# Projection bias as a plain load added by VectorE, last two norms' sums by accumulating operations with squares on ScalarE

## The chip, the cores and the metric

The kernel runs on one core of one Trainium2 chip. The metric is device time in microseconds (us), each version beside the kernel before on the same chip. TensorE is called PE in profiles, PEld is its weight load, VectorE is DVE, ScalarE is ACT, GpSimd is POOL, SyncE is SP.

## The reference, cut to what matters

128 samples of 128 rows by 512 columns go through a max over a small graph product and a norm, then through attention with 8 heads, a projection with bias, a norm, a residual, and a last norm:

```python
x = _layernorm(x + relu_max(adj, x, b))            # layer 0: "first norm"
qkv = x @ w_qkv                                    # 12 "products" per group of 4 samples
o = softmax(mask(q k^T * scale)) v @ w_proj + b_proj
ln = (o - mu) * rsqrt(var + eps) * ln_gamma + ln_beta
x = _layernorm(x + o + ln)                         # needs the sums of o, then of x + o + ln
```

In these inputs `b_proj` and `ln_beta` are zero and `ln_gamma` is one, but a general kernel must apply them.

## The kernel before

A group is four samples; there are 32. TensorE does a **dense stretch** (products 4 to 11, which give q and k, and one projection), then an **attention stretch** (scores, transposes, attend, projections, and the v products). Every operation has a place in a plan, in us. TensorE and ScalarE run in exactly the plan's order; the order on VectorE, GpSimd and SyncE is left to the scheduler. To **evacuate** a product is to read it out of the buffer that TensorE wrote it to (a PSUM buffer), so that the next product can use it: ScalarE reads the main part, then VectorE adds the rest. A wait in an engine's queue holds up what stands behind it: in group 13 below ScalarE is idle for 2.49 us while a finished product stands behind the operation that waits.

```python
def projected_main(b):                       # ScalarE evacuates the main part
    os[b] = work.tile([P, D], FP, tag="o", bufs=4, ...)
    nc.scalar.activation(os[b], pps["o", b][0], AF.Copy, scale=1.0 + 1.0 / HALF)   # last group: VectorE
def projected_rest(b):
    nc.vector.tensor_tensor(os[b], os[b], pps.pop(("o", b))[1], op=ALU.add)
def bias(b):                                 # GpSimd: accumulating DMA
    nc.gpsimd.dma_start(os[b], row(b_proj), accum_op=ALU.add)
def residual_beta(b):                        # xb: 3 buffers, loaded with x by SyncE before
    nc.gpsimd.dma_start(xbs[b], row(ln_beta), accum_op=ALU.add)
def residual_o(b):
    nc.gpsimd.dma_start(xbs[b], os[b], accum_op=ALU.add)
def stats(mv, src, name):                    # VectorE
    nc.vector.bn_stats(st, src)
    nc.vector.bn_aggr(mv, st)
# then GpSimd: add eps, power -0.5; VectorE: norm_1; stats again; ScalarE: norm_2; store
def dense_main(g, j):                        # evacuation of product j: ScalarE, then VectorE
    nc.scalar.activation(dense_to(g, j), pps[g, j][0], AF.Copy, scale=1.0 + 1.0 / HALF)
def dense_rest(g, j):
    nc.vector.tensor_tensor(dst, dst, pps.pop((g, j))[1], op=ALU.add)
# [cut: loads, splits into high and low parts, softmax, plan]
```

## Time and profile before

| | before |
|---|---|
| median, fastest to slowest of 3 | 2183.7 us, 2180.96 to 2185.78 |
| TensorE busy | 2073.4 us, 95% |
| group 2's start, 28 groups from there, the rest | 146.6, 1867.2, 177.3 us |
| mean group | 66.69 us |

All but the first row are of the profiled execution, which took 2192.8 us, 0.4% above the median.

The busy shares make TensorE the bound. What is left to win without taking matmuls away lies in its idle gaps and in matmuls that run slowly after a gap. The prediction shows the lines and reads them.

### The profile page before, as it was taken

The numbers are of one execution on the slowest core, as the hardware profiler recorded it, in microseconds if no ns is written. First come the engines' busy times: TensorE is split into PE (matmuls) and PEld (weight loads), VectorE is DVE, ScalarE is ACT, GpSimd is POOL, SyncE is SP. The second block draws the span as 40 slices with busy tenths as digits, with TensorE's granted clock in tenths as the row PEclk, the third lists the DMA queues.
The fourth block names the chain that finished last, engine by engine and source line by source line (L and its number), as shares of the span: only waits on it lengthen the run. The fifth ranks groups of instructions, "written<-read, shape, count | busy, mean of one in ns | idle before, by whom it ended". The sixth has DMA issues, their size and how long they took to land.

```text
span 2191.1 us, 34777 instructions
## 1 busy us (share of the span) xinstructions
PE 2073.4 (95%) x12033; PEld 1612.2 (74%) x12033; DVE 1726.7 (79%) x2747; ACT 1334.3 (61%) x3742; POOL 719.0 (33%) x1325
## 2 busy tenths in 40 slices
PE   7899999999999999999999999999999999999986
PEld 5677777777777777777777777777777777777764
DVE  7688777887778887778877788877788877788876
ACT  5756565665656666666656566666566666566652
POOL 2122334323343233343223332333332233332334
PEclk8999999999999999999999999999999999999998
DMA  5135455344554454554444544544544454544443
GB/s 179 58 71 118 110 121 121 82 107 111 120 117 90 114 119 111 121 121 86 113 111 116 124 87 111 119 114 116 127 90 107 119 113 120 129 90 102 104 99 90
DMA packets 134000, 239.85 MB, mean 109 GB/s; under 512 B 14656, under 2 KB 18880, under 8 KB 133824
## 3 DMA queue, kind: packets, MB, share of 16 engines
q0 software_dynamic: 54144, 98.59, 27.5%
q1 hardware_dynamic: 79392, 138.97, 19.6%
q8 instruction: 95, 1.56, 0.3%
q14 instruction: 81, 0.66, 0.1%
q10 hardware_dynamic: 288, 0.07, 0.0%
HBM read 137.95 MB, written 67.11 MB: 94 GB/s over the span
## 4 chain that ended last, share of the span: by engine, by line
PE 47%; DMA 18%; POOL 13%; DVE 10%; ACT 7%; issue 5%; POOLq 0%; SPq 0%; DVEq 0%; ACTq 0%
DMA o<-in_L_gnn_b_proj_dram 14%; PE psc L324 5%; ACT e L346 4%; PE ppt L361 4%; DMA xb<-x 3%; POOL rstd L168 3%; PE pav L374 3%; PE pa L189 2%; PE ptx L245 2%; POOL xb L418 2%; POOL ve L166 2%; DVE o L432 2%; POOL ssq L227 1%; DVE st L179 1%; POOL sum L213 1%
## 5 line engine op out<-in xcount | busy, mean ns | idle before, releaser
L346 ACT ACTIVATE e<-e,nmax 128x128 f32<-128x128 f32 x1024 | 395.6, 390 | 1.6 <-DVE nmax L339 1.5
L410 POOL DMA_DIRECT2D o<-in_L_gnn_b_proj_dram x124 | 114.4, 923 | 633.7 <-DVE o L405 609.2
L418 POOL DMA_DIRECT2D xb<-o x124 | 110.2, 889 | 428.1 <-DMA o<-in_L_gnn_b_proj_dram 428.1
L432 DVE SCALAR_TENSOR_TENSOR o<-o,rstd,xb 128x512 f32<-128x512 f32 x128 | 96.0, 750 | 175.7 <-POOL rstd L168 175.5
L365 ACT COPY eT<-ppt 128x1024 f32<-128x1024 f32 x128 | 128.9, 1007 | 127.8 <-PE ppt L361 127.8
L265 ACT CAST x_h<-xh 128x512 fp32r<-128x512 f32 x128 | 79.4, 621 | 188.9 <-DVE xh L253 188.3
L346 ACT ACTIVATION_READ_ACCUMULATOR e<-e,nmax 128x1 f32 x1024 | 193.9, 189 | 0.0
L389 POOL DMA_DIRECT2D xb<-in_L_gnn_ln_beta_dram x128 | 119.2, 931 | 224.4 <-DMA xb<-x 111.0
L331 DVE SCALAR_TENSOR_TENSOR e<-psc,mask 128x1024 f32<-128x1024 f32 x128 | 156.0, 1219 | 43.9 <-PE psc L324 43.9
L234 ACT ACTIVATE xt<-xt,sum,ssq 128x512 f32<-128x512 f32 x128 | 97.1, 805 | 139.1 <-POOL sum L228 139.1
L179 DVE BATCH_NORM_STATS2 st<-o 128x6 f32<-128x512 f32 x256 | 173.3, 678 | 9.5 <-DMA o<-in_L_gnn_b_proj_dram 6.2
L218 ACT ACTIVATE square<-xt,sum 128x512 bf16<-128x512 f32 x128 | 92.1, 719 | 115.4 <-POOL sum L213 113.4
L361 PEld LDWEIGHTS ppt<-ident,e 128*128 128x128 f32 x1024 | 119.8, 141 | 52.4 <-issue 46.5
L355 DVE TENSOR_TENSOR e<-e,sums 128x1024 f32<-128x1024 f32 x128 | 155.4, 1214 | 0.1
L339 DVE TENSOR_REDUCE nmax<-e 128x8 f32<-128x1024 f32 x128 | 154.8, 1209 | 0.0
L168 POOL TENSOR_TENSOR rstd<-ve,mhalf 128x1 f32<-128x1 f32 x256 | 150.4, 589 | 10.5
L324 PE MATMUL psc<-qkT 64*128 64x128 f32 x2048 | 149.1, 285 | 2.7 <-DVE qkT L313 2.7
L324 PEld LDWEIGHTS psc<-qkT 64*128 64x128 f32 x2048 | 124.4, 188 | 25.9 <-issue 15.6
L374 PE MATMUL pav<-eT,v 128*64 128x128 f32 x2048 | 140.1, 279 | 1.2 <-ACT eT L365 1.2
L374 PEld LDWEIGHTS pav<-eT,v 128*64 128x64 f32 x2048 | 109.2, 136 | 41.9 <-issue 29.0
L189 PE MATMUL pa<-xt,adjT 128*128 128x512 f32 x256 | 135.6, 616 | 0.4 <-DVE adjT L99 0.4
L361 PE MATMUL ppt<-ident,e 128*128 128x128 f32 x1024 | 132.9, 273 | 0.5 <-DVE qkT L313 0.5
(4652 smaller groups left out, 5681.8 us busy)
## 6 DMA issues: line engine op xcount, KB each, us to landing
xt<-in_x_dram SPq DMA_DIRECT2D x128, 256.0 KB, 2.9
x<-xt SPq DMA_DIRECT2D x128, 256.0 KB, 2.6
xb<-x SPq DMA_DIRECT2D x128, 256.0 KB, 3.5
xb<-in_L_gnn_ln_beta_dram POOLq DMA_DIRECT2D x128, 256.0 KB, 5.5
out_dram<-o SPq DMA_DIRECT2D x128, 256.0 KB, 3.8
o<-in_L_gnn_b_proj_dram POOLq DMA_DIRECT2D x124, 256.0 KB, 4.2
xb<-o POOLq DMA_DIRECT2D x124, 256.0 KB, 3.3
wraw<-in_L_gnn_w_qkv_dram SPq DMA_DIRECT2D x12, 256.0 KB, 3.7
```

Source lines behind the costliest of these rows:

```text
L168: nc.gpsimd.tensor_tensor(r, ve, mhalf[:, :n], op=ALU.pow)
L179: nc.vector.bn_stats(st, src)
L189: nc.tensor.matmul(pa[b], adjT, xs[b], start=True, stop=True)
L324: nc.tensor.matmul(psc[:, s, hp, :], qkT[hs, hp, i, :], qkT[hs, KC + hp, i, :], start=True, stop=True,)
L331: nc.vector.scalar_tensor_tensor(e, pscs.pop(b).rearrange("p s a m -> p (s a) m"), scale, mask_b, op0=ALU.mult, op1=ALU.add,)
L339: nc.vector.tensor_reduce(nmax, es[b], AX.X, ALU.max, negate=True)
L346: nc.scalar.activation(e[:, j, :], e[:, j, :], AF.Exp, bias=nmax[:, j : j + 1], accum_out=sums[:, j : j + 1],)
L355: nc.vector.tensor_tensor(e, e, sums[:, :, None].to_broadcast([P, H, P]), op=ALU.mult)
L361: nc.tensor.transpose(ppts[b][:, j, :], e[:, j, :], ident)
L374: nc.tensor.matmul(pavs[b][s * HD : (s + 1) * HD, hp, :], v[:, h * HD : (h + 1) * HD], eT[:, s * HP + hp, :], start=True, stop=True,)
L418: nc.gpsimd.dma_start(xbs[b], os[b], accum_op=ALU.add)
L432: nc.vector.scalar_tensor_tensor(o, o, norms.pop((b, 1)), xbs.pop(b), op0=ALU.mult, op1=ALU.add,)
```

## The change

Intent: take the bias off GpSimd's queue, which stands still until each accumulating load has landed, and take the statistics off VectorE. The sum comes with an operation that runs anyway, and the sum of squares is made by ScalarE as (sum - 512 x)^2, so no mean is needed first. The norms get new places.

```diff
-    def projected_main(b):   # ScalarE copy, bias later by GpSimd
+    def bias(b):
+        os[b] = work.tile([P, D], FP, tag="o", bufs=4, name=f"o_{b}")
+        nc.sync.dma_start(os[b], row(b_proj))
+    def projected_main(b):
+        nc.vector.scalar_tensor_tensor(
+            os[b], pps["o", b][0], 1.0 + 1.0 / HALF, os[b], op0=ALU.mult, op1=ALU.add)
     def projected_rest(b):
-        nc.vector.tensor_tensor(os[b], os[b], pps.pop(("o", b))[1], op=ALU.add)
+        add_sum(b, 1, pps.pop(("o", b))[1], 1.0, os[b])      # same, with accum_out
+    def squares(x, s):
+        nc.scalar.activation(square, x, AF.Square, bias=s[:, 0:1], scale=-float(D), accum_out=s[:, 1:2])
+    def deviation(s, n):                                     # GpSimd
+        nc.gpsimd.tensor_scalar(s, s, float(D) ** -3, EPS, op0=ALU.mult, op1=ALU.add)
+        nc.gpsimd.tensor_tensor(s, s, mhalf[:, :n], op=ALU.pow)
-    stats_1, stats_2 by bn_stats and bn_aggr                 # [cut]
+    stats(b, 1), stats(b, 2) by squares and deviation        # [cut]; the first norm's too
-        at(u + 3.0, bias, b)
+        at(u - 5.0, bias, b)
 # [cut: keep_0, mean_0, rstd_0, load_bias]
-                at(u + 9.0 + 1.0 * i, norm_0, b + i)
+                at(u + 14.0 + 1.5 * i, norm_0, b + i)
-                u = t + (10.0 + 5.0 * i if g < NG - 1 else (4.0, 9.0, 14.0, 27.6)[i])
-                normed((g - 2) * G + i, u, u + 2.0, u + 3.5, u + 6.0)
+                u = t + 1.0 + 4.5 * i
+                normed((g - 2) * G + i, u, u + 3.0, u + 6.0, u + 9.0)
```

The four arguments of `normed` after the sample are the places of the first statistics, norm_1, the second statistics and norm_2. For the fourth sample of a group (i = 3), norm_2 now stands at t + 23.5.

More of the change, by code (lines that the diff above doesn't have):

```diff
@@ L81, in tile_adj_resnorm_d2 @@
     pps, qkTs, vs, pscs, es, ppts, eTs = {}, {}, {}, {}, {}, {}, {}
-    pavs, oTs, xbs, os, mv1s, norms = {}, {}, {}, {}, {}, {}
+    pavs, oTs, xbs, os, sums_of, norms = {}, {}, {}, {}, {}, {}
     def load_x(b):
@@ L161, in load_gamma @@
         nc.sync.dma_start(gamma_sb, row(ln_gamma))
-    def norm_of(mv, n, name):
-        ve = small.tile([P, n], FP, tag=f"ve{n}", name=f"ve_{name}")
-        nc.gpsimd.tensor_scalar(ve, mv[:, :, 1], EPS, None, op0=ALU.add)
-        r = small.tile([P, n], FP, tag=f"rstd{n}", name=f"rstd_{name}")
-        nc.gpsimd.tensor_tensor(r, ve, mhalf[:, :n], op=ALU.pow)
-        return r
-    def shift_of(mv, r, n, name):
-        nm = small.tile([P, n], FP, tag=f"nm{n}", name=f"nm_{name}")
-        nc.gpsimd.tensor_scalar(nm, mv[:, :, 0], -1.0, None, op0=ALU.mult)
-        nc.gpsimd.tensor_tensor(nm, nm, r, op=ALU.mult)
-        return nm
-    def stats(mv, src, name):
-        st = small.tile([P, 6], FP, tag="bnst", name=f"st_{name}")
-        nc.vector.bn_stats(st, src)
-        nc.vector.bn_aggr(mv, st)
     def conv(b):
@@ L203, in add_0 @@
         if i == 0:
-            mv0s[g] = [small.tile([P, G], FP, tag=f"{n}0", bufs=2, name=f"{n}0_{g}") for n in ("sum", "ssq")]
+            mv0s[g] = small.tile([P, G, 3], FP, tag="sum0", bufs=2, name=f"sum0_{g}")
         nc.scalar.activation(
-            xs[b], xs[b], AF.Identity, bias=rms[g][:, i : i + 1], accum_out=mv0s[g][0][:, i : i + 1],
+            xs[b], xs[b], AF.Identity, bias=rms[g][:, i : i + 1], accum_out=mv0s[g][:, i, 0:1],
         )
-    def mean_0(b, n):
-        g, i = divmod(b, G)
-        m = mv0s[g][0][:, i : i + n]
-        nc.gpsimd.tensor_scalar(m, m, -1.0 / D, None, op0=ALU.mult)
     def stats_0(b):
         g, i = divmod(b, G)
-        nc.scalar.activation(
-            square, xs[b], AF.Square, bias=mv0s[g][0][:, i : i + 1],
-            accum_out=mv0s[g][1][:, i : i + 1],
-        )
+        squares(xs[b], mv0s[g][:, i, :])
     def rstd_0(b, n):
         g, i = divmod(b, G)
-        nmean, ssq = (m[:, i : i + n] for m in mv0s[g])
-        nc.gpsimd.tensor_scalar(ssq, ssq, 1.0 / D, EPS, op0=ALU.mult, op1=ALU.add)
-        nc.gpsimd.tensor_tensor(ssq, ssq, mhalf[:, :n], op=ALU.pow)
+        total, ssq, nmean = (mv0s[g][:, i : i + n, k] for k in range(3))
+        nc.gpsimd.tensor_scalar(nmean, total, -1.0 / D, None, op0=ALU.mult)
+        deviation(ssq, n)
         nc.gpsimd.tensor_tensor(nmean, nmean, ssq, op=ALU.mult)
@@ L393, in project @@
         product(("o", b), b % G != 0, lambda kc: [(f[:, kc, :], w[:, kc, :]) for f, w in parts])
+    def bias(b):
+        os[b] = work.tile([P, D], FP, tag="o", bufs=4, name=f"o_{b}")
+        nc.sync.dma_start(os[b], row(b_proj))
     def projected_main(b):
-        os[b] = work.tile([P, D], FP, tag="o", bufs=4, name=f"o_{b}")
-        if b < B - G:
-            nc.scalar.activation(os[b], pps["o", b][0], AF.Copy, scale=1.0 + 1.0 / HALF)
-        else:
-            nc.vector.scalar_tensor_tensor(
-                os[b], pps["o", b][0], 1.0 + 1.0 / HALF, xs["bias"], op0=ALU.mult, op1=ALU.add,
-            )
-    def projected_rest(b):
-        nc.vector.tensor_tensor(os[b], os[b], pps.pop(("o", b))[1], op=ALU.add)
-    def bias(b):
-        if b < B - G:
-            nc.gpsimd.dma_start(os[b], row(b_proj), accum_op=ALU.add)
-    def load_bias():
-        xs["bias"] = xpool.tile([P, D], FP, tag="xt", name="bias")
-        nc.sync.dma_start(xs["bias"], row(b_proj))
+        nc.vector.scalar_tensor_tensor(
+            os[b], pps["o", b][0], 1.0 + 1.0 / HALF, os[b], op0=ALU.mult, op1=ALU.add,
+        )
+    def projected_rest(b):
+        add_sum(b, 1, pps.pop(("o", b))[1], 1.0, os[b])
     def residual_o(b):
@@ L418, in residual_o, with add_sum, stats @@
             nc.gpsimd.dma_start(xbs[b], os[b], accum_op=ALU.add)
-    def stats_1(b):
-        mv1s[b] = small.tile([P, 1, 2], FP, tag="mv1", name=f"mv1_{b}")
-        stats(mv1s[b][:, 0, :], os[b], f"1_{b}")
-        norms[b, 1] = norm_of(mv1s[b], 1, f"1_{b}")
+    def add_sum(b, n, in0, scalar, in1):
+        s = sums_of[b, n] = small.tile([P, 3], FP, tag=f"sum{n}", name=f"sum{n}_{b}")
+        nc.vector.scalar_tensor_tensor(
+            os[b], in0, scalar, in1, op0=ALU.mult, op1=ALU.add, accum_out=s[:, 0:1],
+        )
+        nc.gpsimd.tensor_scalar(s[:, 2:3], s[:, 0:1], -1.0 / D, None, op0=ALU.mult)
+    def squares(x, s):
+        nc.scalar.activation(
+            square, x, AF.Square, bias=s[:, 0:1], scale=-float(D), accum_out=s[:, 1:2],
+        )
+    def deviation(s, n):
+        nc.gpsimd.tensor_scalar(s, s, float(D) ** -3, EPS, op0=ALU.mult, op1=ALU.add)
+        nc.gpsimd.tensor_tensor(s, s, mhalf[:, :n], op=ALU.pow)
+    def stats(b, n):
+        s = sums_of[b, n]
+        squares(os[b], s)
+        deviation(s[:, 1:2], 1)
+        if n == 2:
+            nc.gpsimd.tensor_tensor(s[:, 2:3], s[:, 2:3], s[:, 1:2], op=ALU.mult)
     def norm_1(b):
-        o = os[b]
+        o, s, xb = os[b], sums_of.pop((b, 1)), xbs.pop(b)
         if b >= B - G:
-            nc.vector.tensor_tensor(xbs[b], xbs[b], o, op=ALU.add)
+            nc.vector.tensor_tensor(xb, xb, o, op=ALU.add)
         nc.vector.scalar_tensor_tensor(
-            o, o, mv1s.pop(b)[:, 0, 0:1], gamma_sb, op0=ALU.subtract, op1=ALU.mult,
+            o, o, s[:, 2:3], gamma_sb, op0=ALU.add, op1=ALU.mult,
         )
-        nc.vector.scalar_tensor_tensor(
-            o, o, norms.pop((b, 1)), xbs.pop(b), op0=ALU.mult, op1=ALU.add,
-        )
-    def stats_2(b):
-        mv = small.tile([P, 1, 2], FP, tag="mv2", name=f"mv2_{b}")
-        stats(mv[:, 0, :], os[b], f"2_{b}")
-        rstd = norm_of(mv, 1, f"2_{b}")
-        norms[b, 2] = rstd, shift_of(mv, rstd, 1, f"2_{b}")
+        add_sum(b, 2, o, s[:, 1:2], xb)
     def norm_2(b):
         o = os.pop(b)
-        rstd, nm = norms.pop((b, 2))
-        nc.scalar.activation(o, o, AF.Identity, bias=nm, scale=rstd)
+        s = sums_of.pop((b, 2))
+        nc.scalar.activation(o, o, AF.Identity, bias=s[:, 2:3], scale=s[:, 1:2])
         nc.sync.dma_start(out[b], o)
@@ L463, in normed @@
         at(u - 4.0, residual_o, b)
-        at(u, stats_1, b)
+        at(u, stats, b, 1)
         at(v, norm_1, b)
-        at(w, stats_2, b)
+        at(w, stats, b, 2)
         at(z, norm_2, b)
@@ L529, in beside_dense @@
                 at(u + 5.0 + 0.9 * i, stats_0, b + i)
-            at(u + 4.5, mean_0, b, G)
-            at(u + 8.0, rstd_0, b, G)
+            at(u + 8.7, rstd_0, b, G)
             for i in range(G):
-                at(u + 9.0 + 1.0 * i, norm_0, b + i)
-                at(u + 10.0 + 1.0 * i, keep_0, b + i)
+                at(u + 14.0 + 1.5 * i, norm_0, b + i)
+                at(u + 15.0 + 1.5 * i, keep_0, b + i)
         for i in range(G):
@@ L549, in tile_adj_resnorm_d2 @@
         at(u + 2.9, add_0, b)
-        at(u + 3.3, mean_0, b, 1)
         at(u + 3.6, stats_0, b)
@@ L568, in tile_adj_resnorm_d2 @@
     at(places[3 * KC - 1], load_gamma)
-    at(PERIOD * (NG - 1), load_bias)
     t = 0.0
```

## The prediction

> **What bounds the kernel now.** I read the page's busy shares first, then who waited for whom, then one group of four samples in order of time, then a table by stage.
>
> ```profile
> PE 2073.4 (95%) x12033; PEld 1612.2 (74%) x12033; DVE 1726.7 (79%) x2747; ACT 1334.3 (61%) x3742; POOL 719.0 (33%) x1325
> ...
> POOL xb L418 <- DMA o<-in_L_gnn_b_proj_dram: 428.1, 124, 5.0
> ...
> DVE o L432 <- POOL rstd L168: 175.5, 93, 4.9
> ACT xt L234 <- POOL sum L228: 139.1, 31, 5.2
> ...
> ACT square L218 <- POOL sum L213: 113.4, 33, 4.9
> ```
>
> TensorE is busy 95% of the span, so there is little to win unless its busy time itself is inflated. The waits show a chain that starts at a transfer: GpSimd adds the projection bias with an accumulating DMA (line 410), then issues the residual DMA that reads the result (line 418), and for that it stands still until the bias has landed: 428.1 / 124 = 3.45 us each time. Everything behind it in GpSimd's queue, the small mean and rstd operations, is late; VectorE waits for rstd and ScalarE for the sums.
>
> Does it reach TensorE? Group 15 in order of time says yes:
>
> ```profile
> 1034.42 0.87 POOL L418 DMA_DIRECT2D xb<-o  x1 [4.62 <-DMA o<-in_L_gnn_b_proj_dram]
> ...
> 1037.15 0.53 POOL L168 TENSOR_TENSOR rstd<-ve,mhalf 128x1 f32<-128x1 f32 x1
> ...
> 1039.01 0.75 DVE L432 SCALAR_TENSOR_TENSOR o<-o,rstd,xb 128x512 f32<-128x512 f32 x1 [4.66 <-POOL rstd L168]
> ...
> 1040.40 0.67 DVE L313 TENSOR_TENSOR qkT<-qkT,pp_(15, 6)_10008 128x512 f32<-128x512 f32 x1
> ...
> 1041.13 0.76 PE L278 MATMUL pp_(15, 10)_10140<-x_h,w_h 128*128 128x512 f32 x1 [3.42 <-DVE qkT L313]
> 1041.69 0.63 PE L279 MATMUL pp_(15, 10)_10140<-x_l,w_l 128*128 128x512 f32 x1
> ```
>
> Read it downwards: GpSimd waits 4.62 us for the bias, so rstd comes late, so VectorE's norm waits 4.66 us, so the evacuation of product 6 is late, so product 10, which needs its PSUM buffer, keeps TensorE idle 3.42 us. Then the next matmuls follow each other at 0.43 us (1041.69 to 1042.12) where undisturbed ones take 0.233 us (1035.68 to 1035.91): the stall is paid twice.
>
> By stage, for an undisturbed attention stretch between two dense stretches:
>
> ```profile
> 952.20:979.80 27.60, 25.86 (x110) 20.39 (x109) 18.99 (x35) 17.83 (x45) 15.39 (x30) 1.00 0.55 123
> 979.80:1017.50 37.70, 37.70 (x268) 29.25 (x267) 33.93 (x51) 23.33 (x73) 6.31 (x11) 1.00 0.46 107
> 1017.50:1048.30 30.80, 27.38 (x110) 21.52 (x109) 19.34 (x35) 17.82 (x45) 16.90 (x34) 0.94 0.54 127
> ...
> 146.60:2013.80 1867.20, 1802.34 (x10531) 1405.70 (x10529) 1482.56 (x2353) 1153.00 (x3249) 625.71 (x1148) 0.99 0.49 111
> ```
>
> Columns: window, its length, then busy time of PE, PEld, DVE, ACT, POOL, the clock, DMA share, GB/s. The attention stretch is pure TensorE: 37.70 busy of 37.70. The dense stretch is not: 27.6 to 30.8 us long for at least 25.86 us of matmuls (nine products of twelve matmuls at 0.233 = 25.2, plus the 0.7 that the first one takes longer). From the first matmul of group 2's dense stretch (146.6) to group 30's (2013.8) lie 28 groups in 1867.2 us, 66.69 each; the floor is 25.86 + 37.70 = 63.56. So 28 x 3.13 = **87.5 us** are lost, of which 1867.2 - 1802.3 = 64.9 is idle TensorE and the other 22.6 us slow matmuls. Group 30 loses another 1.6. That is the whole pool from which this change can gain in the steady part: about 89 us, 4.1% of 2183.7.
>
> **What the Trainium skill says.** (1) "DMA: Bandwidth & Descriptors", section on the anatomy of one DMA from GpSimd: DMA engines do not wait on semaphores, the wait happens on the issuing sequencer before dispatch. The trace agrees: line 418's wait is GpSimd's own idle time. The same section fits about 2.0 us + bytes/436e3, 2.6 us for 256 KB; the trace's median for the bias is 4.2 us, and that decides. (2) "TensorE: Matmul & The Clock Gate", Part 1: an idle window of about 3.4 us halves the clock. The trace agrees: after 3.42 us idle the spacing nearly doubled, while after 1.74 us (group 14, product 10) it stayed at 0.23. (3) "ScalarE: Activation LUTs", rules for kernel authors: about 0.3 us per ACTIVATE plus 0.83 ns an element, 0.72 us for 512; the squares on line 218 take 0.719. (4) "VectorE: DVE Perf Modes", section on two Vector instructions with no wait between them: an operation that also writes out its accumulator is two instructions. No VectorE operation of this kernel does so; on ScalarE the read shows as 0.19 us of its own.
>
> **The change, part by part.** Consecutive records overlap, so I count by the distance between starts.
>
> *Bias.* Removed: 124 accumulating DMAs on GpSimd with 0.92 us of issue each (114 us, 3.7 per group), and with them line 418's 428 us of waiting. Added: 128 plain loads of the same 256 KB on SyncE, five places ahead of the product. A plain load from DRAM lands in 2.9 to 3.7 us in the trace, so each should be there in time, and DMA engines are at some 45% share.
>
> *Evacuation.* 124 copies leave ScalarE (0.5 us apart: 2.0 us per group) and go to VectorE as the scalar_tensor_tensor that the last group has now (line 400, 0.69 long, 0.60 apart): +2.4 us per group.
>
> *Statistics.* VectorE loses 8 bn_stats and 8 bn_aggr per group, 0.61 + 0.10 apart: -5.7 us. It gains 8 accumulator reads; I estimate 0.1 us of spacing each, as bn_aggr has: +0.8. VectorE net: 2.4 - 5.7 + 0.8 = -2.5, from 52.9 (19.0 + 33.9 above) to 50.4 us of a 63.56 us group. ScalarE gains 8 squares at 0.85 us (square and read): +6.8, less 2.0, so 41.2 to 46.0 us per group. Nearly all of the 6.8 falls in the dense stretch, where it goes from 17.8 to about 24 of 25.9 us. GpSimd's small operations stay about as many.
>
> *First norm.* The squares no longer wait for a mean from GpSimd (113 us of ScalarE waits at line 218; 4 waits of 0.34 to 0.80 at the start, which I take as 1.5 us off the start). norm_0 moves five places later, so rstd has more time before ScalarE's fixed order reaches it.
>
> None of the saved work is itself on the path, because TensorE sets the end. What counts is that GpSimd stops blocking. A product can be evacuated about 11.2 - 2.8 - 0.6 = 7.8 us late before TensorE notices (four products of PSUM buffers at 2.8 us, less its own product and evacuation), so waits of 2 or 3 us that remain cost nothing.
>
> What can remain: three xb buffers serve four samples, so the fourth's residual load, beta (5.5 us) and residual_o (3.3 us) come one after another inside the dense stretch, and GpSimd still waits there for beta to land. I estimate 0.4 us of TensorE time per group, 12 us in all. The last 115 us have 12 us of idle TensorE in waits on other engines; the bias leaves most of it, the squares add ScalarE hops to it: 0.
>
> Sum: 2183.7 - 89 + 12 - 1.5 = 2105; I say **2106 us**, 3.6% faster.
>
> **Rivals.** *ScalarE becomes the bound of the dense stretch.* For it: about 24 of 25.9 us, in a fixed order that now holds waits for VectorE and GpSimd between the evacuations of the products. Against: by my count of its order it falls some 3.5 us behind by the middle and catches up before the end, inside the 7.8 us. If it fails, each group keeps 1 to 2 us of stall: 2135 to 2160. *Another wait replaces the bias wait on GpSimd.* For it: beta is still accumulated, line 389 already waits 111 us for the residual load, and residual_o now follows beta alone. If half of the stall stays: about 2145. *VectorE in the attention stretch becomes late*, 33.9 of 37.7 busy and three more evacuations in it, or waiting for a bias that SyncE issued late. Against: the statistics of earlier samples leave that stretch, and the projection's PSUM buffer is needed again some 4 us after its evacuation (1007.1 to 1011.5). Half a microsecond in each of four places would cost 60 us and eat most of the gain. *The transfer was hidden anyway*, as the 5% idle TensorE suggests: group 15's chain speaks against it.
>
> **Range and chances.** Floor: all stalls gone and 3 us more at the ends, about 2090. The upper end, 2142, has some 60% of the loss left in place. The 2% line lies at 2140. One strong mechanism, shown in nearly every group, against three rivals that would each have to bring back over half: faster 0.87, within 2% 0.11, slower 0.02.
>
> **What would show it.** Line 418's wait for the bias gone, the idle time before rstd's users down to a third; the dense stretches all within 1 us of 25.9, attention still at 37.7; VectorE near 1650 us busy, ScalarE near 1480, GpSimd near 620. ScalarE's squares waiting, with TensorE waiting for evacuations of products 8 to 11, would show the first rival; GpSimd waiting on the beta transfer with rstd late again, the second; TensorE idle in the attention stretch, the third.

## The result, and the profile after

The changed kernel takes 2147.51 us (median of 4 runs, 2145.23 to 2150.08) against 2184.74 us for the kernel before (median of the 4 runs beside it). The ratio is **0.9831** (95% interval 0.981 to 0.9851): 1.7% faster, within the 2% that counts as the same, and 5 us above the predicted range. Ratios are the mean time of one kernel's runs over that of the other's in the same rounds, so they are not quite the ratios of these medians.

Busy shares of the whole span:

```profile
PE 2059.5 (96%) x12033; PEld 1602.7 (75%) x12033; DVE 1623.6 (76%) x2615; ACT 1453.9 (68%) x4130; POOL 640.8 (30%) x1329
```

The work moved as planned: VectorE 103 us lighter, ScalarE 120 us heavier, GpSimd 78 us lighter. The wait for the bias transfer is gone. The waits that now matter (who waited for whom: us in total, times, longest):

```profile
DVE qkT L284 <- ACT qkT L280: 208.3, 127, 4.3
ACT o L420 <- POOL sum L406: 198.4, 96, 4.9
...
PE psc L295 <- DVE qkT L284: 50.0, 31, 3.2
```

`psc` is the scores product and `qkT` the evacuated q and k, so a wait at the scores has taken the place of the wait at product 10. By stage (window, length, busy time of PE, PEld, DVE, ACT, POOL, clock, DMA share, GB/s), group 13's dense and attention stretch, and the 28 groups:

```profile
861.60:887.20 25.60, 25.60 (x110) 20.39 (x109) 15.78 (x31) 21.57 (x57) 14.84 (x33) 1.00 0.53 129
887.20:926.60 39.40, 37.96 (x268) 29.28 (x268) 33.99 (x51) 23.17 (x74) 4.76 (x9) 1.00 0.41 104
...
142.60:1979.40 1836.80, 1790.61 (x10531) 1397.11 (x10529) 1393.38 (x2241) 1254.60 (x3585) 552.29 (x1148) 0.99 0.46 113
```

The dense stretch is pure TensorE now, 25.60 of 25.60. But the attention stretch, untouched before at 37.70, has grown to 39.40. A group takes 1836.8 / 28 = 65.60 us, 1.09 less than before. Of the profiled span's 43.0 us gain, 4.0 come before group 2, 30.4 from the 28 groups, and 8.6 after. (The medians differ by only 37.2 us, because the profiled execution of the kernel before was a long one; its 66.69 us a group may be too high by 0.3, an estimate: 8.1 us over 28 groups.)

Where the stretches meet in group 13, in order of time (start, length, engine, line, operation, idle time before it):

```profile
886.98 0.96 POOL L360 DMA_DIRECT2D xb<-in_L_gnn_ln_beta_dram  x1 [0.29 <-issue]
...
888.15 0.20 ACT L392 ACTIVATION_READ_ACCUMULATOR square<-o,sum 128x1 f32 x1
...
889.25 0.86 POOL L360 DMA_DIRECT2D xb<-in_L_gnn_ln_beta_dram  x1 [1.31 <-DMA xb<-x]
...
890.18 0.19 POOL L398 TENSOR_SCALAR sum<-sum 128x1 f32<-128x1 f32 x1
...
891.09 0.19 POOL L406 TENSOR_TENSOR sum<-sum 128x1 f32<-128x1 f32 x1
891.32 0.81 ACT L420 ACTIVATE o<-o,sum 128x512 f32<-128x512 f32 x1 [2.49 <-POOL sum L406]
892.04 0.57 ACT L280 ACTIVATE qkT<-pm_(13, 11)_8471 128x512 f32<-128x512 f32 x1
...
892.65 0.69 DVE L284 TENSOR_TENSOR qkT<-qkT,pd_(13, 11)_8472 128x512 f32<-128x512 f32 x1 [3.10 <-ACT qkT L280]
...
893.39 0.49 PE L295 MATMUL psc<-qkT 64*128 64x128 f32 x4 [1.44 <-DVE qkT L284]
```

ScalarE has the squares of the fourth sample ready at 888.35. GpSimd should turn them into a deviation, but a beta transfer stands ahead in its queue, waits for the residual load and takes its issue time, so the deviation starts at 890.18. On ScalarE that sample's norm_2 stands next but one, after product 10's evacuation, so ScalarE waits 2.49 us. Only then comes the evacuation of product 11, which was finished at 887.41. VectorE follows, and TensorE, which has already done 12 of its 16 score matmuls, waits 1.44 us for the last part of q and k. Group 13 is the rule: in every group from 2 to 30 a beta issue stands directly ahead of this deviation on GpSimd, which starts 1.3 to 3.0 us after the squares are ready.

How late is too late? Over groups 3 to 29, I took from the trace the start of VectorE's evacuation of product 11, counted from that product's end, and the wait at the scores. In group 9 they are 4.75 and 0.96 us, in group 3 5.31 and 1.53, in group 7 6.25 and 2.46. In 20 of the 27 groups the wait is the delay less **3.8 us**, within 0.03 us; in the other seven it is shorter than that by up to 1.5 us. In the kernel before, the same evacuation starts 0.11 us after the product's end in every group, as here in group 14 (product 11 ends at 980.00):

```profile
980.11 0.69 DVE L313 TENSOR_TENSOR qkT<-qkT,pd_(14, 11)_9503 128x512 f32<-128x512 f32 x1
```

Some waits cost double. In groups 5, 7, 18, 22, 24 and 28 TensorE's busy time in the attention stretch is 39.4 to 39.6 us where other groups have 38.0: for a few microseconds after the wait the matmuls are nearly twice as far apart, and the granted clock of group 18's stretch is 0.96 where group 13's is 1.00. Group 18 shows it: a wait of 1.78 us, and then matmuls 0.43 us apart (1223.68 to 1224.11) instead of 0.23.

```profile
1219.98 0.49 PE L295 MATMUL psc<-qkT 64*128 64x128 f32 x4 [1.78 <-DVE qkT L284]
...
1223.68 0.63 PE L249 MATMUL pm_(18, 1)_11723<-w_h,x_h 128*128 128x512 f32 x1
1224.11 0.63 PE L250 MATMUL pm_(18, 1)_11723<-w_l,x_l 128*128 128x512 f32 x1
```

So the 28 groups lose 1836.8 - 28 x 63.30 = 64 us against a floor that the experiments show to be 63.30 us a group: 46 idle, 18 slow.

### The profile page after: what moved, and what is told of

It reads as the page before. It is cut to its first block, busy times and chain, and to the rows that moved or that the text cites. A ratio compares the mean times of both kernels' runs of the same rounds, so it can differ in the third digit from the quotient of the medians. Undisturbed runs are those within 1.5% of the kernel's fastest.

```text
span 2148.1 us, 34985 instructions
## 1 busy us (share of the span) xinstructions
PE 2059.5 (96%) x12033; PEld 1602.7 (75%) x12033; DVE 1623.6 (76%) x2615; ACT 1453.9 (68%) x4130; POOL 640.8 (30%) x1329
## 5 line engine op out<-in xcount | busy, mean ns | idle before, releaser
L388 POOL TENSOR_SCALAR sum<-sum 128x1 f32<-128x1 f32 x256 | 68.8, 269 | 1109.3 <-DVE o L385 1109.2
L420 ACT ACTIVATE o<-o,sum 128x512 f32<-128x512 f32 x128 | 104.2, 814 | 198.7 <-POOL sum L406 198.4
L399 POOL TENSOR_TENSOR sum<-sum,mhalf 128x1 f32<-128x1 f32 (+1 forms) x291 | 206.5, 710 | 24.1
L295 PE MATMUL psc<-qkT 64*128 64x128 f32 x2048 | 157.6, 288 | 50.0 <-DVE qkT L284 50.0
L412 DVE SCALAR_TENSOR_TENSOR o<-o,sum,gamma_sb 128x512 f32<-128x512 f32 x128 | 97.0, 758 | 129.5 <-ACT square L392 123.9
L392 ACT ACTIVATE square<-o,sum 128x512 bf16<-128x512 f32 x256 | 182.5, 713 | 14.7 <-DVE o L385 12.8
L385 DVE SCALAR_TENSOR_TENSOR o<-o,sum,xb 128x512 f32<-128x512 f32 x128 | 96.0, 750 | 107.0 <-POOL sum L399 106.8
L360 POOL DMA_DIRECT2D xb<-in_L_gnn_ln_beta_dram x128 | 125.1, 981 | 82.8 <-DMA xb<-x 69.3
L345 PE MATMUL pav<-eT,v 128*64 128x128 f32 x2048 | 144.4, 285 | 1.1 <-ACT eT L336 1.1
L398 POOL TENSOR_SCALAR sum<-sum 128x1 f32<-128x1 f32 (+1 forms) x291 | 90.4, 311 | 159.3 <-ACT square L392 144.5
```

The source lines that it names most:

```text
L295: nc.tensor.matmul(psc[:, s, hp, :], qkT[hs, hp, i, :], qkT[hs, KC + hp, i, :], start=True, stop=True,)
L345: nc.tensor.matmul(pavs[b][s * HD : (s + 1) * HD, hp, :], v[:, h * HD : (h + 1) * HD], eT[:, s * HP + hp, :], start=True, stop=True,)
L392: nc.scalar.activation(square, x, AF.Square, bias=s[:, 0:1], scale=-float(D), accum_out=s[:, 1:2],)
L399: nc.gpsimd.tensor_tensor(s, s, mhalf[:, :n], op=ALU.pow)
```

## The experiments

Theory: a fixed order on ScalarE puts a norm that waits for GpSimd ahead of the evacuation of product 11, and the scores need that evacuation within 3.8 us. Rivals: ScalarE simply has too much work in the dense stretch; VectorE is late; or the gain and loss belong to other parts of the change. All eight kernels gave the reference's result.

### One norm later on ScalarE

```diff
-                normed((g - 2) * G + i, u, u + 3.0, u + 6.0, u + 9.0)
+                normed((g - 2) * G + i, u, u + 3.0, u + 6.0, u + (9.0 if i < G - 1 else 13.0))
```

> Changed kernel with one edit: the last norm of the fourth sample of a group goes 4 places later in ScalarE's fixed order, behind the evacuation of product 11. Theory (in the changed kernel the first scores of a group wait for product 11, whose evacuation stands behind that norm, which waits for GpSimd): TensorE's wait at the scores falls from 50 us to under 15, mean period from 65.6 to about 64.2, time about 2107. Rival (ScalarE simply has too much work in the dense stretch): only the norm's own 0.7 us per group is won, about 20 us, time about 2127. Second rival (the chain through VectorE sets it, order on ScalarE does not matter): 2140 or more.

Measured: **2091.78 us** (2091.68 to 2095.92), ratio 0.9561 to the kernel before. The edit removes no work. The wait at the scores fell from 50.0 us to 0.3 us in all; evacuation of product 11 starts 2.28 us after the product's end on average, where it was 5.51. The group is 63.82 us. The 28 groups, and ScalarE's wait at norm_2:

```profile
142.80:1929.70 1786.90, 1775.57 (x10531) 1387.53 (x10529) 1392.86 (x2241) 1255.77 (x3586) 554.87 (x1148) 1.00 0.47 116
```

```profile
ACT o L420 <- POOL sum L406: 161.1, 96, 4.8
```

ScalarE still waits 161.1 us at norm_2, but no longer with product 11 behind it. What remains are 11 us of TensorE waits at the attend product, whose input ScalarE now copies after that norm. The theory's number for the group was 64.2 and for the time 2107; the ends gave more than expected, with 160.0 us from group 30 on instead of 168.7. Load as the cause is refuted: ScalarE's busy time, 1455.3 us, is the same as in the changed kernel.

### No beta transfers

```diff
-        at(u - 10.0, residual_beta, b)
```

Right only because `ln_beta` is zero here.

> Changed kernel without the accumulating load of ln_beta (which is zero in these inputs, so the result stays right; not a general kernel). Theory that GpSimd's queue is held up by the beta transfers, and ScalarE by GpSimd: ScalarE's wait at the last norm falls from 198 us to under 80, TensorE's wait at the scores from 50 us to under 15, time about 2105. Rival that ScalarE's own work is the bound: waits at the norm fall but the scores still wait over 30 us, time 2130 or more.

Measured: **2076.51 us** (2075.99 to 2077.01), ratio 0.9487. The 28 groups, in the same columns, and ScalarE's wait at norm_2:

```profile
142.00:1914.40 1772.40, 1772.40 (x10531) 1388.55 (x10529) 1395.86 (x2241) 1260.78 (x3585) 463.75 (x1036) 1.00 0.37 100
```

```profile
ACT o L420 <- POOL sum L406: 67.8, 95, 1.6
```

TensorE never stops: 1772.40 busy of 1772.40, 63.30 us a group, with ScalarE as loaded as before (1260.78 us). ScalarE's wait at the norm fell from 198.4 to 67.8 us. So in the changed kernel it is the beta transfers, through GpSimd's queue, that make norm_2 late, and norm_2's place that lets this reach TensorE; taking away either cures it. The edit also takes 128 transfers off the DMA engines (share 0.37 for 0.46), so that the queue is the link, and not the traffic, rests on the lines of group 13 and their repetition in every group.

### The bias part alone

```diff
 # kernel before, with [cut: the last group's own bias load]:
-            nc.scalar.activation(os[b], pps["o", b][0], AF.Copy, scale=1.0 + 1.0 / HALF)
+        nc.vector.scalar_tensor_tensor(
+            os[b], pps["o", b][0], 1.0 + 1.0 / HALF, os[b], op0=ALU.mult, op1=ALU.add)
-            nc.gpsimd.dma_start(os[b], row(b_proj), accum_op=ALU.add)
+        os[b] = work.tile([P, D], FP, tag="o", bufs=4, name=f"o_{b}")
+        nc.sync.dma_start(os[b], row(b_proj))
-        at(u + 3.0, bias, b)
+        at(u - 5.0, bias, b)
```

> Kernel before with the bias part alone: plain load into the output tile, evacuation by VectorE, bn_stats kept, old places. Theory that the gain comes from freeing GpSimd of the bias wait: the stalls at product 10 (64 us of idle TensorE) shrink to under a third and ScalarE stays at 39 us a group, time 2105 to 2130, so better than the whole change. Rival that VectorE is too full with three more evacuations in the attention stretch: over 2145.

Measured: **2094.25 us** (2092.1 to 2094.92), ratio 0.9566: better than the theory's range and 53 us faster than the whole change. Group 13's dense and attention stretch and the 28 groups:

```profile
844.00:869.60 25.60, 25.60 (x111) 20.41 (x110) 18.59 (x34) 16.64 (x40) 12.41 (x27) 1.00 0.52 126
869.60:907.30 37.70, 37.70 (x270) 29.22 (x268) 36.12 (x56) 22.75 (x74) 6.12 (x10) 1.00 0.43 111
147.70:1920.90 1773.20, 1773.04 (x10530) 1389.66 (x10529) 1530.42 (x2465) 1104.64 (x3137) 519.51 (x1036) 1.00 0.46 117
```

TensorE is busy 1773.04 of 1773.20 us. VectorE holds 36.12 of the 37.70 us attention stretch without delaying it, so the rival of a full VectorE falls. The bias part alone wins everything that stalls and slow matmuls had cost in the steady groups. It is two edits that no run separates, the load that leaves GpSimd and the copy that leaves ScalarE. That the first carries the gain is read from the waits: VectorE's longest wait for rstd is 2.1 us, where it was 4.9.

```profile
DVE o L423 <- POOL rstd L168: 114.2, 94, 2.1
```

The part wins nothing at the start (147.7 us to group 2) and 8 us at the end (169.4 from group 30 on).

### The statistics part alone

The changed kernel with the old bias path: ScalarE's copy and the accumulating load on GpSimd. The sum then lacks the bias, which is zero here.

```diff
 # changed kernel, with [cut: the last group's own bias load]:
-        nc.sync.dma_start(os[b], row(b_proj))
+            nc.gpsimd.dma_start(os[b], row(b_proj), accum_op=ALU.add)
-        nc.vector.scalar_tensor_tensor(...)      # projected_main
+            nc.scalar.activation(os[b], pps["o", b][0], AF.Copy, scale=1.0 + 1.0 / HALF)
-        at(u - 5.0, bias, b)
+        at(u + 3.0, bias, b)
```

> Changed kernel with the old bias path (ScalarE copy, accumulating load on GpSimd; the sum is then taken without the bias, which is zero in these inputs, so the result stays right). Theory: the 3.5 us waits on GpSimd are back and now reach ScalarE's fixed order as well, time 2180 or more. Rival that the statistics and the new places bring the gain: 2150 or less.

Measured: **2254.14 us** (2252.91 to 2258.23), ratio 1.0305, slower than the kernel before. The waits that carry it:

```profile
POOL xb L388 <- DMA o<-in_L_gnn_b_proj_dram: 323.2, 93, 4.5
ACT o L428 <- POOL sum L414: 262.9, 105, 6.3
...
PE psc L295 <- DVE qkT L284: 53.6, 27, 3.3
```

GpSimd waits for the bias again, ScalarE for GpSimd, and TensorE waits both at the scores and at product 0, 62.9 us there. With the bias on GpSimd the new statistics and places lose 66 us against the kernel before beside them (median 2188.47 us). ScalarE starts product 11's evacuation 8.1 us after the product's end on average, where the changed kernel has 4.9 and the kernel before starts it 0.9 us ahead of the end: the squares and the new places have put ScalarE, with its fixed order, into the chain that GpSimd holds up.

### The changed kernel with the old places

```diff
 # [cut: rstd_0, keep_0]
-                at(u + 14.0 + 1.5 * i, norm_0, b + i)
+                at(u + 9.0 + 1.0 * i, norm_0, b + i)
-                u = t + 1.0 + 4.5 * i
-                normed((g - 2) * G + i, u, u + 3.0, u + 6.0, u + 9.0)
+                u = t + (10.0 + 5.0 * i if g < NG - 1 else (4.0, 9.0, 14.0, 27.6)[i])
+                normed((g - 2) * G + i, u, u + 2.0, u + 3.5, u + 6.0)
```

> The changed kernel with the places of the kernel before (norms 10 + 5 per sample, first norm 9 + 1). Theory that the loss sits in the order on ScalarE: the fourth sample's last norm stands at 31, behind product 11's evacuation at 24.3, so the wait at the scores mostly goes, though norms then mix with the attention stretch: 2100 to 2130. Rival that the new places were needed against GpSimd's waits: over 2150.

Measured: **2349.7 us** (2342.32 to 2353.58), ratio 1.0742: I missed by over 200 us. The wait at the scores did go, and a larger one came:

```profile
ACT square L392 <- DVE o L385: 253.2, 97, 7.5
...
DVE o L412 <- DMA xb<-o: 216.8, 29, 9.6
...
PE pav L345 <- ACT eT L336: 206.9, 30, 8.9
```

With the old places the fourth sample's squares stand on ScalarE ahead of the copy `eT` that the attend product (`pav`) needs. They wait for VectorE's norm_1, which waits for the residual transfer, so TensorE stands still up to 8.9 us once per group. I read this from the waits and did not test it further. By that reading it is the same mechanism in another spot: once the squares are on ScalarE, a late sample holds up what stands behind it. So the squares could not stay at the old places, and the new ones stopped 4 us of plan short for one norm.

### Can the ends be had as well?

Three kernels build on the bias part alone, which left the start and the end. The first adds the first norm's squares of the raw sum:

```diff
 # [cut: the rest of the first norm]
-        m = mv0s[g][0][:, i : i + n]
-        nc.gpsimd.tensor_scalar(m, m, -1.0 / D, None, op0=ALU.mult)     # mean_0, before the squares
+        squares(xs[b], mv0s[g][:, i, :])
```

> The bias part alone plus the first norm's part (squares of the raw sum, no wait for a mean from GpSimd), bn_stats for the last two norms, old places. Theory that the changed kernel's 4.9 us earlier group 2 (142.8 against 147.7 us) comes from the first norm's part: start of group 2 at about 143, period unchanged at 63.3, time about 2089. Rival that it comes from the places or from VectorE's lighter load: 2094 as for the bias part alone.

Measured: 2093.92 us (2093.39 to 2094.52), ratio 0.9577. Group 2 starts at 145.8 us, so this part brings at most 1.9 of the 4.9 us (one profile each; the next kernel, with the same start, has 144.5), and the end took 2.4 us longer, for a reason that I did not find. A miss for the theory. The traces show where most of the rest lies: from group 0's first product to group 2's it takes 106.1 to 106.7 us in the five kernels with the old places of the first norm and 103.3 to 103.6 in the five with the new ones, whatever their other parts.

The second uses the new statistics for the last two groups only:

```diff
+    LATE = B - 2 * G
+        if b < LATE: nc.vector.tensor_tensor(os[b], os[b], rest, op=ALU.add)
+        else: add_sum(b, 1, rest, 1.0, os[b])      # and squares, deviation in stats_1 and stats_2
```

> The one before, with the accumulated sums and ScalarE squares for the last two groups of four samples only. Theory that these statistics pay only where TensorE has stopped being the bound and VectorE is the fuller engine: the stretch from group 30 on falls from 169.4 to about 161 us, period 63.3, time 2076 to 2082, the best of all. Rival that the tail's gain was in the places, not the statistics: 2087 or more.

Measured: 2083.92 us (2082.39 to 2085.29), ratio 0.953. The stretch from group 30 on fell from 171.8 to 163.0 us with the places unchanged, so the statistics do pay there. The total is 2 us over the expected 2076 to 2082: the start was 144.5 us and not 143, and the end 163.0 and not 161.

The third takes the changed kernel's places at both ends, and nowhere else, and the new statistics for the last three groups:

```diff
+    LATE = B - 3 * G
+            late, step = (14.0, 1.5) if g == 0 else (9.0, 1.0)               # norm_0
+                else:                                                        # last group
+                    u = t + 1.0 + 4.5 * i
+                    normed((g - 2) * G + i, u, u + 3.0, u + 6.0, u + (9.0 if i < G - 1 else 13.0))
```

> The one before with both ends taken from the changed kernel: new statistics from the last three groups on, with that kernel's places in the last group (and the fourth sample's last norm late), and its places of the first norm in group 0 alone. Theory that the ends are additive: group 2 starts at about 143 us, 28 periods of 63.3, about 160 us from group 30 on, 2077 in all, the best general version. Rival that the places of one end disturb the steady part: 2084 or more.

Measured: **2077.42 us** (2076.51 to 2079.01), ratio 0.9504, as expected. The three parts of the span:

```profile
0.00:142.80 142.80, 122.61 (x628) 90.55 (x629) 110.23 (x173) 94.31 (x258) 22.22 (x43) 0.93 0.37 110
142.80:1916.70 1773.90, 1773.10 (x10529) 1389.78 (x10528) 1531.00 (x2465) 1105.16 (x3137) 531.67 (x1036) 1.00 0.47 117
1916.70:2076.00 159.30, 142.48 (x878) 112.06 (x876) 124.90 (x211) 99.28 (x273) 64.38 (x134) 0.98 0.47 113
```

It is a general kernel, 5% faster than the kernel before and 3.3% than the changed one (2077.42 / 2147.51 = 0.967, of medians from different jobs). With 0.8 us of idle TensorE left in 28 groups, waits there have nothing more to give.

| kernel | us | 28 groups, each | to group 2 | from group 30 |
|---|---|---|---|---|
| before | 2183.7 | 66.69 | 146.6 | 177.3 |
| the change | 2147.5 | 65.60 | 142.6 | 168.7 |
| one norm later | 2091.8 | 63.82 | 142.8 | 160.0 |
| no beta transfers | 2076.5 | 63.30 | 142.0 | 160.4 |
| bias part alone | 2094.3 | 63.33 | 147.7 | 169.4 |
| statistics part alone | 2254.1 | 68.87 | 142.8 | 180.1 |
| the change, old places | 2349.7 | 72.52 | 145.7 | 175.4 |
| bias part, first norm's squares | 2093.9 | 63.36 | 145.8 | 171.8 |
| the same, late statistics | 2083.9 | 63.33 | 144.5 | 163.0 |
| both ends | 2077.4 | 63.35 | 142.8 | 158.9 |

## Why the prediction was wrong

**Right: the bias transfer stalls TensorE through GpSimd** (that the gain belongs to GpSimd's wait and not to ScalarE's copy is read from waits, as said above). The bias part alone took the group from 66.69 to 63.33 us. The pool was even a little larger than the predicted 87.5 us: the floor is 63.30 and not 63.56, because the 0.7 us extra of the first matmul, which I had counted as work, shrank to 0.4. So it is 28 x 3.39 = 95 us.

**Right: the work of each engine, nearly.** VectorE 1623.6 us for "near 1650", ScalarE 1453.9 for "near 1480", GpSimd 640.8 for "near 620". The accumulator read, which I took as 0.1 us of spacing, costs next to nothing on VectorE: an evacuation with it is followed by the next operation after 0.61 us (862.40 to 863.01) where one without takes 0.60. ScalarE's squares were counted at 0.85 us, square and read; from start to next start they take 0.71, and 0.72 in the trace before (9.39 to 10.11).

**Right: the dense stretches.** From group 2 to 29 they are 25.6 to 26.0 us, bar one of 27.0. And the projection's evacuation did not make the attention stretch late through VectorE: TensorE did idle in that stretch, which the prediction had named as the sign of its third rival, but VectorE only passed on ScalarE's delay there, as the later norm on ScalarE shows.

**The step that failed: "A product can be evacuated about 11.2 - 2.8 - 0.6 = 7.8 us late before TensorE notices".** That sum counts PSUM buffers, and holds where the buffer is the only hurry: in the kernel before, the wait at product 10 is the delay of product 6 less 7.68 us in every group from 2 to 30. Product 11 has another reader: the scores, only one product and one set of transposes later. Its slack is 3.8 us by the trace. VectorE started on it 5.5 us after its end on average, inside the 7.8 and outside the 3.8. What was built on that step failed with it: "waits of 2 or 3 us that remain cost nothing" (norm_2's wait of 2.0 to 3.7 us in these groups did cost), the 0.4 us per group that remain, which were 65.60 - 63.30 = 2.3, and the verdict on the first two rivals, whose delays I had seen and called harmless. Nor did ScalarE catch up before the end, as the prediction had it: it started products 8, 9 and 11 some 4.7 to 4.9 us after their ends. The kernel before hid this deadline, with an evacuation 0.11 us after the end. Its stall at product 10 may be part of the reason: the bias part alone, which has no such stall but more work on VectorE, starts it 2.4 us after the end, still inside the 3.8. The new place of norm_2 took it past that, as the later norm shows.

**Which rival came.** The second in substance: another wait, that of the beta issue for the residual load, took the bias wait's place on GpSimd, as line 389's waits had shown. The prediction looked for GpSimd waiting until beta had landed; that wait is 23.9 us in the whole changed kernel, the one for the residual load 69.3. The first only in form: ScalarE runs late, but by waiting in a fixed order, not by load, since without the beta transfers the same load fits.

**The ends.** I gave them 1.5 us; they brought 12.6, and with the norm in its later place 3.8 + 17.3. A slip without effect: at the upper end, 2142 us, some 55% of the loss is left (49 of 89 us), not 60.

**"After 1.74 us (group 14, product 10) it stayed at 0.23"** led me to think that waits under 2 us are not paid twice. In the changed kernel some are, as group 18 after 1.78 us. The trace before already had such cases: groups 22 and 24 fell to 0.43 us after 1.83 and 1.80 us, while group 19 kept 0.23 after 2.27.

## What to carry to other kernels

Work out slack per consumer, not per buffer: the last product before a stage that reads them all has the shortest deadline, and a kernel that meets it easily does not show it. When an operation moves to an engine with a fixed order, ask what stands behind each wait that it brings; the gain here sat in one norm that stood 0.8 us of plan ahead of a deadline. Test the parts of a compound change alone: here one part was worth 4.3%, the other cost 3% without it, and together they gave 1.7%.

## What the Trainium skill lacked or had wrong

- "TensorE: Matmul & The Clock Gate", Part 1, ties the halved clock to an idle window of about 3.4 us that runs freely, and tells of short idle times between matmul groups that also make it swing, without their length. In the changed kernel a wait of 1.78 us at the scores (group 18) was followed by matmuls 0.43 us apart, while most groups with waits of 1.4 to 1.8 us kept 0.23, and group 15 kept it after 2.29; 6 of 28 groups paid. Neither the page nor a run here says which short waits are paid.
- "VectorE: DVE Perf Modes", section on two Vector instructions with no wait between them, says that an operation with an accumulator output is two instructions, and the trace agrees. It gives no cost: 0.08 us as recorded, about 0.01 us of spacing.
- "DMA: Bandwidth & Descriptors", anatomy of one DMA from GpSimd, has a fit that gives an estimate of 2.6 us for 256 KB. Accumulating loads of that size landed after 4.2 us (bias, before), 5.5 us (beta, before) and 6.7 us (beta, after), the accumulating transfer of `o` into `xb` after 3.3 us in both; the page has no figure for accumulating ones.
- "Perfetto Trace Analysis", optimization strategy, says that a gap repeating on the engine that should be saturated can mean too few buffers. Before the change it did (product 10 and its PSUM buffer); after it the gap repeated as regularly, 31 times, for a data deadline that no buffer count shows. The page says how to follow a gap back through its semaphores; no page tells how to find such a deadline before it is missed. Here it was the delay less the wait, 3.8 us.
